# Three groups of routed pairs instead of two, tile sums on GpSimd, and a last chunk spread over all of PSUM, in a two-layer transformer kernel

## The chip, the cores and the metric

One core of a Trainium2 chip runs the whole program. The metric is the device time of one execution in microseconds; lower is better. The engines of the core are TensorE (PE in the profile, with its weight loads shown as PEld), VectorE (DVE), ScalarE (ACT), GpSimd (POOL) and SyncE (SP, which here only issues transfers). Each engine works through its own list of instructions in order.

## The reference, cut to what matters

The input x has 4 sequences of 1024 tokens with 256 values each, in float32. Two layers follow each other, each an attention-like part and a part with 8 experts, each part wrapped in a normalization with a scale and a shift, and added back through a gate. The change lies in layer 1:

```python
h = layernorm(x) * (1 + ca) + sa
x = x + ga * fast_weight(h)                 # chunks of 128 tokens, one after the other: the weights of
                                            # a chunk are those of the chunk before times a decay
h = layernorm(x) * (1 + cb) + sb
logits = h @ router_w.T                     # 8 experts
probs = softmax(logits); topk_vals, topk_idx = top_k(probs, 2)
topk_w = topk_vals / (topk_vals.sum(-1) + 1e-6)
expert_out = einsum('nh,eho->eno', h, expert_weights)           # 256 x 256 for each expert
x = x + gb * sum over the two chosen (expert_out[chosen] + probs[chosen]) * topk_w
```

The decay of a chunk needs the mean squared error of the chunk before, so the chunks of the fast-weight part are a chain. Only two of eight experts count for a token, so the kernel computes, for most tokens, only those two.

## The kernel before, in words

A sequence of 1024 tokens is 8 chunks of 128; a chunk has one tile of 128 tokens by 256 values for each of the 4 sequences, so layer 1 has 8 chunks of 4 tiles. For each chunk c the function `fast` computes the fast-weight part: 32 matmuls of 512 columns (`p_u`, line 2007), a SiLU on ScalarE (line 2019) and a product on VectorE (line 2023), 32 matmuls of 256 columns (`p_f`, line 2055), and per tile a step that GpSimd adds to x (line 2103). `normal` then normalizes the chunk (statistics and the modulation of line 1618 on VectorE, scaling on ScalarE at line 1608) and transposes it on TensorE (`pm_t`, line 1660). `routed` computes the 8 logits (`pm_e`, line 188; `pm_l`, line 2150) and, on VectorE, the two best experts.

Pairs of a token and a chosen expert are then sorted by expert in **groups**. Group `ga` takes chunks 0 to 3 (16 tiles), group `gb` chunks 4 to 6 (12 tiles); the last chunk, 7, is not sorted. When the last chunk of a group is routed, `closed` counts the pairs of each expert (`pm_turn`, `pm_total`, `pm_bases`, `pm_rank`, `pm_blocks` on TensorE, small operations on VectorE and ScalarE). Each expert's pairs are cut into blocks of 128 rows, with a fixed number of blocks for a group of n tiles:

```python
def blocks_of(n):
    return 2 * n + E - 1
```

That is 39 blocks for `ga` and 31 for `gb`. A block (function `block`) finds its rows (`reach`, `look` and `find`: lines 752, 765 and 778 to 787), gathers them from DRAM through an indirect transfer that GpSimd issues (`xg`, line 347), transposes them (`pm_x`, line 2298), copies them out (line 2304), multiplies them with one expert's weights (`p_e`, line 2315), copies the product out (`y`, line 2325) and stores it to DRAM on SP's queue (line 2328). When all blocks of a group are stored, `combine` gathers for each tile of the group the two products of each token (`yg`, line 347, two indirect transfers for one tile), scales the first on ScalarE (line 1544), adds the second, multiplies by the gate and adds the result to x, all three on VectorE (lines 1550, 1553 and 1555). When the four tiles of a chunk are done, SP stores the chunk (line 2503, 512 KB).

The last chunk goes through `dense`: all 8 experts for all its tokens, as 16 slots of two matmuls of 512 columns (line 2363), each slot consumed by two VectorE operations with the routing weights (lines 2379 and 2388), a gate and a sum on VectorE for each tile (lines 2408 and 2409), and a store of 128 KB for each tile (line 2412).

The PSUM memory has 8 banks, divided in three pools: `p1` of 3 banks, `p2` of 2, `pm` of 3. `dense` uses `p1` alone. Five buffers hold gathered tiles (`yg2`), four hold gathered rows (`xg`), three hold products (`y`).

The order of the instructions on each engine is written by a **planner**, the class `Plan`. Every piece of work is given an engine, an estimated cost, the pieces it comes after, the buffers it holds and a rank; `run` plays this through with the estimates, always starting the ready piece of the lowest rank, and emits the pieces in the order in which they began. A rank such as `c + 0.92` is a place in units of a chunk. On the chip each engine then follows its list in order and waits on semaphores where a piece is not ready. The ranks of the groups are written out by hand: `base, span` for the blocks of a group, a pair of numbers for the sums and the stores.

Of the kernel before, what the change touches and what calls it, by code (L numbers as in the profile page):

```python
# [12 lines left out]
ALU = mybir.AluOpType  # L13
# [20 lines left out]
STRIP = 32  # L34
AHEAD = 3
DX = D + 2
W1ROW = KD * H + KH
# [3 lines left out]
class Plan:  # L41
# [6 lines left out]

    LATENCY, PATIENCE, GRACE = 0.12, 0.4, 0.3

    def __init__(self, rings=(), **room):
# [11 lines left out]
    def run(self):  # L63
        room = dict(self.room)
        ring = {kind: [] for kind in self.rings}
        begun, ended, free, held = {}, {}, {}, []
        left = sorted(range(len(self.pieces)), key=lambda i: (self.pieces[i][5], i))
        t = 0.0
        while left:
# [13 lines left out]
            for i in list(left):  # L83
                engine, us, _, after, holds, rank, at, lag = self.pieces[i]
                if any(a not in ended for a in after):
# [3 lines left out]
                    + [  # L89
                        ended[a] + (self.LATENCY if self.pieces[a][0] != engine else 0.0)  # L90
                        for a in after
# [16 lines left out]
                for h in need:  # L108
                    h[2] = True
                    room[h[0]] -= 1  # L110
                    if h[0] in ring:
                        ring[h[0]].append(h)
                begun[i], ended[i] = t, t + us + lag
                free[engine] = t + us
                held += [(t + us + lag + self.LATENCY, i, q) for q in range(len(holds))]
                left.remove(i)
            if left:
                later += [e[0] for e in held if e[0] > t]
                later += [
                    ended[a] + self.LATENCY  # L120
                    for i in left
                    for a in self.pieces[i][3]
                    if a in ended and ended[a] + self.LATENCY > t
                ]
# [15 lines left out]
def adaln_d2_kernel(  # L140
# [1308 lines left out]
    mods1 = [l1.tile([P, B, D], F32, name=f"mod{i}") for i in range(6)]  # L1449
    groups = [Pairs(l1, l1, "ga", 4 * B), Pairs(l1, l1, "gb", 3 * B)]  # L1450
    mod_rows1 = dram.tile([B, 6, D], F32, name="mod_rows1")
# [41 lines left out]

    def combine(key, c, kind, y, g, tile_of, bias, gate, after, rank, at=0.0, stage=None):

        done = []
        for b in range(B):
# [50 lines left out]
            def second(b=b, s=s):  # L1548
                t = made[key, c, b]
                nc.vector.scalar_tensor_tensor(  # L1550
                    t[:, 0, :], t[:, 1, :], g.w[:, 1, s : s + 1], t[:, 0, :], ALU.mult, ALU.add
                )
                nc.vector.tensor_tensor(t[:, 0, :], t[:, 0, :], gate[:, b, :], ALU.mult)  # L1553
                xs = x_sb[:, c, b, :]
                nc.vector.tensor_tensor(xs, xs, t[:, 0, :], ALU.add)  # L1555

            a = plan(ACT, 0.45, first, after=[got[0]], holds=[slot], rank=rank)
            done.append(
                plan(DVE, 1.35, second, after=[got[1], a], holds=[slot], rank=rank + 0.01 * b)
            )  # L1560
        return done

# [772 lines left out]
    def dense(c, slotT, ts, d, x, rank):  # L2335
# [19 lines left out]
        for b in range(B):  # L2355
            last, st = [], plan.slot("step")
            for j in range(E // 2):
                ps = plan.slot("p1")

                def mm(b=b, j=j):  # L2360
                    p1 = made[key, b, j] = psum(ps_1, [P, 2, D], "p1_e")
                    for k in range(KD):
                        nc.tensor.matmul(  # L2363
                            p1,
                            lhsT=made["n2", c, "hT"][:, k, b, :],
                            rhs=ew[:, 2 * j : 2 * j + 2, k, :],
                            start=(k == 0),
                            stop=(k == KD - 1),
                        )
# [47 lines left out]
    last_pairs = Pairs(l1, l1, "gc", B)  # L2417
    lasts = {"decay": [], 0: [], 1: []}
# [3 lines left out]
    stored = {0: [], 1: []}  # L2422
    for g, rows in zip(groups, rows_of):
        for k in range(KD):
            nc.sync.dma_start(rows[g.n * P :, k * P : (k + 1) * P], ones[:1, :])
    for c in range(NC):
# [3 lines left out]
        else:  # L2430
# [18 lines left out]
        slot, slotT, hs, ts = normal(  # L2449
            ("n2", c), c, "2", [[d] for d in sums], (SHB, SCB), 7.65 if c == NC - 1 else c + 0.92, [range(B)]  # L2450
        )
        which = 0 if c < 4 else 1
        if c == NC - 1:
            d, x = routed(last_pairs, c, 0, slotT, ts, 7.46)
            dense(c, slotT, ts, d, x, 8.23)
            continue
        g, first = groups[which], 4 * which
        at = (c - first) * B
# [12 lines left out]
        )  # L2471
        if c in (3, 6):
            lists, experts, slots = closed(g, lasts[which], c + 0.97)
            base, span = ([4.57, 1.5], [7.35, 0.66])[which]
            ys = [
# [12 lines left out]
            for q in range(first, c + 1):  # L2488
# [9 lines left out]
                    [*ys, slots],  # L2498
                    (6.49, 7.89)[which] + 0.2 * (q - first),
                )  # L2500
# [67 lines left out]
```

## Time and profile before

| what | value |
|---|---|
| runs shown | 1120.11 us median of 3 (1119.87 to 1120.88) |
| profiled execution | 1141.97 us, of which the span from first to last instruction is 1140.2 us |
| mean granted TensorE clock in it | 0.986 |
| PE busy | 1086.3 us, 95% of the span |
| DVE busy | 592.0 us, 52% |
| ACT busy | 428.6 us, 38% |
| POOL busy | 422.5 us, 37% |
| last matmul ends | 1126.4 us after the span's start |

The profiled execution is 21.9 us (2.0%) longer than the median of the runs without a profile. Durations below come from that one execution, so sums are made against its span of 1140.2 us.

In the profile a line such as "L347 POOL DMA_INDIRECT" is a group of instructions of one source line on one engine; "[4.21 <-remote]" behind an instruction is the time that its engine sat idle ahead of it, and what ended the wait. "remote" and "another core or an unknown queue" mean that the recorded events name no releaser. For an indirect transfer the duration is the time in which GpSimd issues it, not the time until the data has landed.

### The profile page before, as it was taken

The numbers are of one execution on the slowest core, as the hardware profiler recorded it, in microseconds if no ns is written. First come the engines' busy times: TensorE is split into PE (matmuls) and PEld (weight loads), VectorE is DVE, ScalarE is ACT, GpSimd is POOL, SyncE is SP. The second block draws the span as 40 slices with busy tenths as digits, with TensorE's granted clock in tenths as the row PEclk, the third lists the DMA queues.
The fourth block names the chain that finished last, engine by engine and source line by source line (L and its number), as shares of the span: only waits on it lengthen the run. The fifth ranks groups of instructions, "written<-read, shape, count | busy, mean of one in ns | idle before, by whom it ended". The sixth has DMA issues, their size and how long they took to land. (4 is left out here: it accounts for less than half of the span.)

```text
span 1140.2 us, 18501 instructions
## 1 busy us (share of the span) xinstructions
PE 1086.3 (95%) x6238; PEld 847.0 (74%) x6238; DVE 592.0 (52%) x2308; ACT 428.6 (38%) x1164; POOL 422.5 (37%) x483
## 2 busy tenths in 40 slices
PE   8998999999999999999999999999999999899883
PEld 5894999999999999999988466566576575547641
DVE  7787232222222222222274788975776445888456
ACT  5976333322333323233343343432434235333421
POOL 1000455555555555555543011010044233616452
PEclk8999999999999999999999999999999999999996
DMA  9414549242422415151260312100024223323532
GB/s 321 174 31 103 191 156 302 100 153 75 154 78 75 150 39 192 33 193 40 70 223 27 96 34 83 39 10 19 19 62 129 75 82 103 102 88 107 155 118 93
DMA packets 77693, 122.38 MB, mean 107 GB/s; under 512 B 27340, under 2 KB 57301, under 8 KB 72990
## 3 DMA queue, kind: packets, MB, share of 16 engines
q0 software_dynamic: 31872, 69.68, 19.5%
q1 hardware_dynamic: 44622, 49.92, 13.3%
q10 hardware_dynamic: 1104, 1.58, 0.4%
q8 instruction: 52, 0.85, 0.3%
q14 instruction: 43, 0.35, 0.1%
HBM read 205.25 MB, written 30.22 MB: 207 GB/s over the span
## 5 line engine op out<-in xcount | busy, mean ns | idle before, releaser
L1710 ACT ACTIVATE hid<-p_h,w 128x128 f32<-128x128 f32 x544 | 154.8, 368 | 323.5 <-issue 251.9
L1698 PEld LDWEIGHTS p_h<-xT,w 128*128 128x128 f32 x2176 | 253.2, 192 | 7.2 <-DVE xT L1683 1.9
L1698 PE MATMUL p_h<-xT,w 128*128 128x128 f32 x2176 | 254.7, 275 | 3.1 <-DVE xT L1683 2.7
L1721 PE MATMUL p_y<-w,hid 128*128 128x256 f32 x1088 | 249.0, 382 | 0.2 <-issue 0.2
L2007 PE MATMUL p_u<-hT,a 128*128 128x512 f32 x512 | 232.0, 596 | 2.9 <-ACT hf L2019 1.4
L1721 PEld LDWEIGHTS p_y<-w,hid 128*128 128x128 f32 x1088 | 201.6, 190 | 25.1 <-DMA w<-in_W,g_wrow 0.4
L2007 PEld LDWEIGHTS p_u<-hT,a 128*128 128x128 f32 x512 | 93.5, 190 | 100.5 <-issue 89.7
L347 POOL DMA_INDIRECT w<-in_W,g_wrow x134 | 135.1, 1008 | 77.4 <-ACT hid L1710 46.7
L1683 DVE COPY xT<-pm_x 128x256 f32<-128x256 f32 x68 | 28.8, 424 | 187.0 <-PE pm_x L1678 134.4
L812 POOL DMA_INDIRECT y<-y,g_dest x68 | 69.5, 1022 | 143.5 <-DVE g_reached L752 108.4
L2055 PE MATMUL p_f<-a,hf 128*128 128x256 f32 x512 | 116.7, 380 | 2.0 <-DVE step L2096 1.0
L1732 DVE TENSOR_TENSOR y<-p_y,w 128x256 f32<-128x256 f32 x68 | 28.9, 425 | 166.9 <-PE p_y L1721 160.7
L2055 PEld LDWEIGHTS p_f<-a,hf 128*128 128x128 f32 x512 | 95.9, 190 | 20.8 <-issue 5.9
L347 POOL DMA_INDIRECT xg<-h_rows,g_row x68 | 66.7, 980 | 120.4 <-DVE g_row L787 98.9
L2103 POOL TENSOR_TENSOR x_sb<-x_sb,step 128x256 f32<-128x256 f32 x32 | 24.9, 778 | 205.8 <-DVE step L2096 153.6
L2315 PE MATMUL p_e<-ew,xT 128*128 x280 | 71.5, 386 | 0.8 <-ACT y L2325 0.8
L2019 ACT ACTIVATE hf<-p_u,decay 128x512 f32<-128x512 f32 x56 | 38.2, 685 | 74.9 <-PE p_u L2007 63.5
L347 POOL DMA_INDIRECT xg<-ga_rows,ga_row x39 | 37.3, 956 | 54.1 <-DVE g_hits L778 19.3
L2315 PEld LDWEIGHTS p_e<-ew,xT 128*128 128x128 f32 x280 | 49.0, 190 | 11.0 <-issue 3.8
L2023 DVE SCALAR_TENSOR_TENSOR hf<-p_u,decay,hf 128x512 f32<-128x512 f32 x56 | 41.9, 748 | 25.7 <-PE p_u L2007 14.3
L1618 DVE TENSOR_TENSOR h<-h,mod 128x256 f32<-128x256 f32 x128 | 51.6, 425 | 6.8 <-ACT h L1608 4.1
L2325 ACT COPY y<-p_e 128x256 f32<-128x256 f32 x70 | 26.1, 373 | 51.4 <-PE p_e L2315 19.2
(371 smaller groups left out, 1259.1 us busy)
## 6 DMA issues: line engine op xcount, KB each, us to landing
yg<-y SPq DMA_DIRECT2D x32, 256.0 KB
ga_y<-y SPq DMA_DIRECT2D x39, 128.0 KB
x_sb<-in_x SPq DMA_DIRECT2D x8, 512.0 KB
h_rows<-xn SPq DMA_DIRECT2D x8, 512.0 KB
gb_y<-y SPq DMA_DIRECT2D x31, 128.0 KB
out_x<-x_sb SPq DMA_DIRECT2D x7, 512.0 KB
a<-in_fw SPq DMA_DIRECT2D x6, 512.0 KB
mod<-mod_rows SPq DMA_DIRECT2D x6, 512.0 KB
```

The lines of the kernel that those rows point to most:

```text
L347: return nc.gpsimd.indirect_dma_start(out=dst, out_offset=None, in_=table, in_offset=bass.IndirectOffsetOnAxis(ap=index, axis=0), bounds_c ...
L812: nc.gpsimd.indirect_dma_start(out=table, out_offset=bass.IndirectOffsetOnAxis(ap=dest, axis=0), in_=y, in_offset=None, bounds_check=2 * s ...
L1618: nc.vector.tensor_tensor(h, h, mods1[(sc, sh)[i]][:, b, :], (ALU.mult, ALU.add)[i])
L1698: nc.tensor.matmul(p1[:, i, :], lhsT=w1[:, k * H + m * P : k * H + (m + 1) * P], rhs=xT[:, k, :], start=(k == 0), stop=(k == KD - 1),)
L1710: nc.scalar.activation(hid[:, m, :], p1[:, i, :], AF.Relu, bias=w1buf[j % 2][:, KD * H + m : KD * H + m + 1],)
L1721: nc.tensor.matmul(p2, lhsT=hid[:, m, :], rhs=w2[:, m * D : (m + 1) * D], start=(m == 0), stop=(m == KH - 1),)
L1732: nc.vector.tensor_tensor(y, p2, w2buf[j % 2][:, KH * D :], ALU.add)
L2007: nc.tensor.matmul(pu, lhsT=a[:, k, m * P : (m + 1) * P], rhs=made["n1", c, "hT"][:, k, :, :], start=(k == 0), stop=(k == KD - 1),)
L2019: nc.scalar.activation(made[key, m], made[key, m, 0], AF.Silu, scale=decays[c])
L2023: nc.vector.scalar_tensor_tensor(h, made[key, m, 1], decays[c], h, ALU.mult, ALU.mult)
L2055: nc.tensor.matmul(made[key, "p2", b], lhsT=made[key, m][:, b * P : (b + 1) * P], rhs=a1[:, m, :], start=(m == 0), stop=(m == KH - 1),)
L2315: nc.tensor.matmul(made[key, "p2"], lhsT=made[key, "xT"][:, k, :], rhs=ew_flat[:, bass.ds(made[key, "at"] + k * D, D)], start=(k == 0), st ...
```

## The change

Five things change, all in layer 1 or in the planner:

1. **Groups.** Chunks 4 to 6 become two groups: `gb` with chunks 4 and 5 (8 tiles, 23 blocks) and `gd` with chunk 6 alone (4 tiles, 15 blocks). There are 77 blocks in place of 70, and a third call of `closed`.
2. **Sums on GpSimd.** In `combine` for layer 1's groups the last addition to x (line 1555) moves from VectorE to GpSimd, as a planned piece of its own; the tile's `yg` buffer is held until it is done.
3. **Last chunk.** The 16 slots of `dense` take their banks in turn from `p1`, `p2` and `pm`.
4. **Ranks.** The ranks of blocks, sums, stores and of the last chunk are replaced by new numbers.
5. **Late messages.** The planner keeps for each piece a time at which the other engines see its end (`seen`). After three or more gathers in a row on GpSimd, a piece of TensorE that ends while they run is taken to be seen later, by 0.5 us for each gather of the row. This alters the planned order only; it adds no instruction.

The diff, cut to its core:

```diff
+N2_LAST, ROUTE_LAST, DENSE = 7.373, 6.892, 8.748
+BLOCKS = ((4.449, 1.589), (6.583, 0.614), (7.627, 0.308))
+SUMS = (6.672, 7.642, 8.45)
+STORES = (5.708, 7.465, 8.095)
+GROUPS = ((0, 1, 2, 3), (4, 5), (6,))
...
+    GATHER, APART, MANY = 1.28, 0.5, 3
...
-                        ended[a] + (self.LATENCY if self.pieces[a][0] != engine else 0.0)
+                        seen[a] + self.LATENCY if self.pieces[a][0] != engine else ended[a]
...
+                seen[i] = ended[i]
+                if engine == "POOL" and us == self.GATHER:
+                    row = row + 1 if t < fetched + self.APART else 1
+                    fetched = t + us
+                elif engine == "PE" and row >= self.MANY and t + us < fetched + self.GATHER:
+                    seen[i] += 0.5 * row
...
-    groups = [Pairs(l1, l1, "ga", 4 * B), Pairs(l1, l1, "gb", 3 * B)]
+    groups = [Pairs(l1, l1, name, len(of) * B) for name, of in zip(("ga", "gb", "gd"), GROUPS)]
...
+        def add(engine, b):
+            xs = x_sb[:, c, b, :]
+            engine.tensor_tensor(xs, xs, made[key, c, b][:, 0, :], ALU.add)
...
                 nc.vector.tensor_tensor(t[:, 0, :], t[:, 0, :], gate[:, b, :], ALU.mult)
-                xs = x_sb[:, c, b, :]
-                nc.vector.tensor_tensor(xs, xs, t[:, 0, :], ALU.add)
+                if y is None:
+                    add(nc.vector, b)
...
-            done.append(
-                plan(DVE, 1.35, second, after=[got[1], a], holds=[slot], rank=rank + 0.01 * b)
-            )
+            d = plan(
+                DVE,
+                1.35 if y is None else 0.93,
+                second,
+                after=[got[1], a],
+                holds=[slot],
+                rank=rank + 0.01 * b,
+            )
+            if y is not None:
+                d = plan(
+                    POOL,
+                    0.76,
+                    lambda b=b: add(nc.gpsimd, b),
+                    after=[d],
+                    holds=[slot],
+                    rank=rank - 0.5,
+                )
+            done.append(d)
...
-                ps = plan.slot("p1")
+                kind = ("p1", "p2", "pm")[(b * E // 2 + j) % 3]
+                ps = plan.slot(kind)
 
-                def mm(b=b, j=j):
-                    p1 = made[key, b, j] = psum(ps_1, [P, 2, D], "p1_e")
+                def mm(b=b, j=j, kind=kind):
+                    bank = {"p1": ps_1, "p2": ps_2, "pm": ps_m}[kind]
+                    p1 = made[key, b, j] = psum(bank, [P, 2, D], f"{kind}_d")
...
-        which = 0 if c < 4 else 1
         if c == NC - 1:
-            d, x = routed(last_pairs, c, 0, slotT, ts, 7.46)
-            dense(c, slotT, ts, d, x, 8.23)
+            d, x = routed(last_pairs, c, 0, slotT, ts, ROUTE_LAST)
+            dense(c, slotT, ts, d, x, DENSE)
             continue
-        g, first = groups[which], 4 * which
+        which = [c in of for of in GROUPS].index(True)
+        g, first = groups[which], GROUPS[which][0]
...
-        if c in (3, 6):
+        if c == GROUPS[which][-1]:
             lists, experts, slots = closed(g, lasts[which], c + 0.97)
-            base, span = ([4.57, 1.5], [7.35, 0.66])[which]
+            base, span = BLOCKS[which]
...
-                    (6.49, 7.89)[which] + 0.2 * (q - first),
+                    SUMS[which] + 0.2 * (q - first),
...
-                plan(SP, 0.1, store, after=done, rank=(6.4, 8.2)[which] + 0.2 * (q - first))
+                plan(SP, 0.1, store, after=done, rank=STORES[which] + 0.2 * (q - first))
```

In the program that the planner writes, TensorE's list is the same up to chunk 4's second half of `p_f`. From there on the blocks of `ga` lie a little differently; the 23 blocks of `gb` lie among the matmuls of chunks 6 and 7 in place of 31 blocks among and behind those of chunk 7; the 15 blocks of `gd` lie among and behind the last `p_f` of chunk 7; and 15 of the 16 dense slots stand at the very end in one row. On GpSimd the 32 gathers of `ga`'s tiles, which stood in one stretch between the row gathers of `ga` and of `gb`, are mixed with the row gathers of `gb`'s blocks and with the new additions; 16 gathers for `gb`'s tiles lie ahead of, among and behind the gathers of `gd`'s rows, and 8 for `gd`'s tiles come last. On SP's queue the stores of finished chunks stand between the stores of block products.

More of the change, by code (lines that the diff above doesn't have):

```diff
@@ L65, in run @@
         ring = {kind: [] for kind in self.rings}
-        begun, ended, free, held = {}, {}, {}, []
+        begun, ended, seen, free, held = {}, {}, {}, {}, []
+        fetched, row = 0.0, 0
         left = sorted(range(len(self.pieces)), key=lambda i: (self.pieces[i][5], i))
@@ L113, in run @@
                 begun[i], ended[i] = t, t + us + lag
+                seen[i] = ended[i]
[4 more added lines that the diff above has]
+                    seen[i] += 0.5 * row
                 free[engine] = t + us
-                held += [(t + us + lag + self.LATENCY, i, q) for q in range(len(holds))]
+                held += [(seen[i] + self.LATENCY, i, q) for q in range(len(holds))]
                 left.remove(i)
@@ L119, in run @@
                 later += [
-                    ended[a] + self.LATENCY
+                    seen[a] + self.LATENCY
                     for i in left
                     for a in self.pieces[i][3]
-                    if a in ended and ended[a] + self.LATENCY > t
+                    if a in seen and seen[a] + self.LATENCY > t
                 ]
@@ L2417, in adaln_d2_kernel @@
     last_pairs = Pairs(l1, l1, "gc", B)
-    lasts = {"decay": [], 0: [], 1: []}
+    lasts = {"decay": [], **{i: [] for i in range(len(GROUPS))}}
     y_of = [dram.tile([g.J * P, D], F32, name=f"{g.name}_y") for g in groups]
@@ L2421, in adaln_d2_kernel @@
     vbs = [l1.tile([P, g.n], F32, name=f"{g.name}_vb") for g in groups]
-    stored = {0: [], 1: []}
+    stored = {i: [] for i in range(len(GROUPS))}
     for g, rows in zip(groups, rows_of):
@@ L2449, in adaln_d2_kernel @@
         slot, slotT, hs, ts = normal(
-            ("n2", c), c, "2", [[d] for d in sums], (SHB, SCB), 7.65 if c == NC - 1 else c + 0.92, [range(B)]
+            ("n2", c), c, "2", [[d] for d in sums], (SHB, SCB), N2_LAST if c == NC - 1 else c + 0.92, [range(B)]
         )
-        which = 0 if c < 4 else 1
         if c == NC - 1:
-            d, x = routed(last_pairs, c, 0, slotT, ts, 7.46)
-            dense(c, slotT, ts, d, x, 8.23)
+            d, x = routed(last_pairs, c, 0, slotT, ts, ROUTE_LAST)
+            dense(c, slotT, ts, d, x, DENSE)
             continue
-        g, first = groups[which], 4 * which
+        which = [c in of for of in GROUPS].index(True)
+        g, first = groups[which], GROUPS[which][0]
         at = (c - first) * B
```

## The prediction

> **What bounds the kernel now.** I read the busy line of the page first, then busy time by stage, then the instructions of the last stages in order of time. I cut stages where TensorE transposes the logits of chunks 5, 6 and 7 (`pm_l`: 959.6, 1012.6 and 1075.7 us), because both programs have these marks. Columns: stretch, its length, then busy us and instructions of PE, PEld, DVE, ACT, POOL, then PE clock, DMA share, GB/s.
>
> ```profile
> PE 1086.3 (95%) x6238; PEld 847.0 (74%) x6238; DVE 592.0 (52%) x2308; ACT 428.6 (38%) x1164; POOL 422.5 (37%) x483
> ```
>
> ```profile
> 848.50:939.90 91.40, 88.31 (x398) 59.63 (x396) 49.01 (x215) 34.99 (x95) 34.19 (x37) 1.00 0.34 98
> 939.90:959.60 19.70, 19.21 (x89) 11.77 (x88) 11.84 (x38) 11.97 (x27) 3.97 (x5) 1.00 0.33 106
> ...
> 1012.60:1075.70 63.10, 56.17 (x288) 39.64 (x286) 42.91 (x215) 23.07 (x68) 30.52 (x33) 1.00 0.38 112
> 1075.70:1126.40 50.70, 42.60 (x113) 21.14 (x113) 29.40 (x83) 12.46 (x29) 25.00 (x26) 0.87 0.38 107
> 1126.40:1140.20 13.80, 0.00 (x0) 0.00 (x0) 8.73 (x22) 0.60 (x1) 0.23 (x1) 0.63 0.33 110
> ```
>
> TensorE bounds all but the end: it is busy 97% of both stretches to 959.6. In the last 64.5 us it has only 42.6 us of work and stops 13.8 us early. The engines in order of time (start, length, engine, line, operation, count, idle before) show why:
>
> ```profile
> 1088.01 19.05 PE L2363 MATMUL p_e<-ew,hT 128*128 128x512 f32 x44
> 1110.78 3.75 PE L2363 MATMUL p_e<-ew,hT 128*128 128x512 f32 x4 [3.72 <-issue]
> 1117.80 6.28 PE L2363 MATMUL p_e<-ew,hT 128*128 128x512 f32 x8 [3.27 <-DVE step L2388]
> ```
>
> ```profile
> 1091.07 0.94 POOL L347 DMA_INDIRECT yg<-gb_y,gb_slot  x1 [10.57 <-DMA gb_y<-y]
> ...
> 1112.79 0.95 POOL L347 DMA_INDIRECT yg<-gb_y,gb_slot  x1 [0.30 <-issue]
> 1119.24 0.94 POOL L347 DMA_INDIRECT yg<-gb_y,gb_slot  x1 [5.51 <-DVE x_sb L1555]
> ```
>
> ```profile
> 1109.63 1.00 DVE L2388 SCALAR_TENSOR_TENSOR step<-p_e,d_w,step 128x256 f32<-128x256 f32 x2 [4.21 <-remote]
> 1116.65 1.00 DVE L2388 SCALAR_TENSOR_TENSOR step<-p_e,d_w,step 128x256 f32<-128x256 f32 x2 [6.02 <-remote]
> ```
>
> ```profile
> 1135.60 0.38 SPq L2503 DMA_DIRECT2D out_x<-x_sb  x1
> ```
>
> The 24 gathers of `gb`'s tiles can start only at 1091.07, when the last of 31 blocks is stored; at 1.25 us each (0.95 and 0.30 of issue) they need 30 us, and each tile then takes VectorE 1.35 us between dense slots. VectorE waits 4.21 and 6.02 us for dense slots whose matmuls lie inside the row that ends at 1107.06: TensorE's messages come late while GpSimd issues 18 gathers in a row. TensorE, three banks ahead at most, idles 3.72 and 3.27 us and then runs at about half clock (3.75 us for a slot that takes 1.72).
>
> **What the Trainium skill says.** "TensorE: Matmul & The Clock Gate", What's actually happening: after an idle window of about 3.4 us the clock falls to half; the trace agrees (gap of 3.72 us, 0.63 granted). "Perfetto Trace Analysis", Tensor Engine Instruction: a matmul's end is a model, and its message to other engines lies outside the window; that fits waits that name no releaser, but says nothing of gathers as their cause. "SBUF — State Buffer", Who interferes with whom: a VectorE operation with two SBUF inputs and a GpSimd operation that reads SBUF exclude each other; line 2103's additions, the same shape as the new ones, take 721 to 977 ns (median 732), which agrees.
>
> **The change, part by part.** Unit prices of TensorE from its rows and the chain of waits: a 512-column matmul 0.87 us (1.74 for two), a 256-column one 0.435, a transpose 0.11, a `look` 0.06.
>
> *Seven more blocks* cost on TensorE 7 x (0.87 + 0.22 + 0.06) = 8.1 us, the third `closed` about 0.4: **+8.5 us, on the path** where TensorE bounds. On GpSimd 7 x 1.25 = 8.8; ScalarE 7 x 0.6 = 4.2; VectorE 7 x 0.8 = 5.6 and some 4 for `closed`; SP seven stores at 0.32. These four lie beside TensorE, which has 111 us in chunks 5 to 7 against some 96 of VectorE and 54 of ScalarE, counted in the same way. If that cover went, VectorE would be next.
>
> *Sums on GpSimd*: 28 times 0.42 leaves VectorE (-11.8 us) and 28 times 0.78 comes to GpSimd (+21.8). In the end stage the four for `gd` leave VectorE's path; elsewhere it gains nothing. Each is a new wait in GpSimd's list, on VectorE's line 1553; row gathers (`xg`) and further `yg` gathers queue behind it, and TensorE's `pm_x` waits for these. Bounds: nothing if VectorE is prompt; 28 waits of about 1.5 us (what a VectorE stretch such as a normalization's root lasts) on the other side. I take nothing while GpSimd has slack, computed next.
>
> *GpSimd's list* from the first `ga` tile (954.4, unchanged, since all of `ga` must be stored) to the last `gd` row gather: 32 of `ga`, 23 rows of `gb`, 10 of `gb`'s tiles, 15 rows of `gd`, 80 gathers by 1.25, and 8 steps and 20 sums by 0.78: 122 us, to 1076, plus some 4 us until `gb`'s lists are known: 1080. TensorE will want that last row at about 1095 (worked out below: the mark at 1091 and a few blocks): 15 us of slack.
>
> *SP's queue*: stores of chunks (0.38) now stand between product stores; a chunk store late for a sum holds products behind it, and three `y` buffers then stop ScalarE's copies. Taken at nothing, since `ga`'s sums come many blocks ahead; 0 to 3 us. The two one-row stores for `gd` at the start lie beside layer 0's work: nothing.
>
> *TensorE by stage*, counting the order: before, 46.9 us of work from chunk 5's `pm_l` to chunk 6's (took 53.0), 51.3 to chunk 7's (63.1), 37.0 after it. After: 63.9, 47.4 and 32.4, 143.7 against 135.2, which is the 8.5 again. Up to chunk 5's mark the sums are equal (123.4 against 123.4), so 959.6 stays. Time over work was 116.1 / 98.2 = 1.18 between the marks of chunks 5 and 7. With **the same 1.18**, 111.3 us of work take 131.4: chunk 7's mark moves from 1075.7 to **1091.0**. Not knowing how the new interleaving packs, I bound the ratio by 1.10 (more matmuls to fill in) and 1.28.
>
> *The end stage*: after that mark 6.3 us of blocks and the first dense slot, then 15 slots by 1.74 = 26.1, and 1.5 for waits: matmuls end at 1124.9. Every slot's bank now has six or more slots before it is needed again, about 10 us, which covers one late message of the size seen. VectorE needs 1.0 for a slot and 0.9 for a tile's end, less than TensorE's 1.74 a slot. The last slot's two operations (1.0), gate and sum (0.86), then a 128 KB store (2.4, as the last `gb_y` store at 1088.7 to the gather it released at 1091.07, and 0.3 of issue): **1129.5**. Beside it the last `gd` product has landed about 1102 (1091.0 + 6.3 + 1.5, copy 0.4, store 2.4); 8 gathers (10.0), 4 sums (3.1), the last pair's landing, scaling and product (3.2) and some 4 us of waits take it to 1122.3, a 512 KB store of 4.6 (1135.60 to the end) to 1126.9, under 3 us short of the path. Were the dense slots quicker, that chain would be next.
>
> Sum: 1129.5 - 1140.2 = -10.7 us of the profiled span (the execution has 1.8 us around it). The runs' median is 21.9 us under the profiled time, and some of the late messages may be smaller there; I take -10: **1110 us**.
>
> **Rivals.**
> - *GpSimd becomes the bound (slower).* Place: the stretch of `gb` and `gd` blocks. If each of 20 sums ahead of the last `gd` row stops its queue by w, the last row comes at 1080 + 20 w. It decides from w = 0.75 us (1095) and has eaten the gain at w = 1.3. At 1.6 us: 1112, 17 late, end 1146.5, +6.3: 1126.4 in the runs. For it: 122 us of work in 141, and GpSimd already waited 5.51 us for line 1555. Against: ready gathers and few waits above 2 us in `ga`'s stretch.
> - *Eaten.* The ratio between the marks rises to 1.28, as late messages still strike mid-chunk (before, ScalarE and VectorE waited up to 6.5 us in `ga`'s row of gathers). 142.5 us, mark 1102.1, end 1140.6: 1120, no change.
> - *Better packing.* Ratio 1.10: mark 1082.0, end 1120.5, -19.7: 1100. For it: `gb`'s blocks get chunk 6's matmuls as filling, where 27 of its 31 blocks before had none, from 1046 on.
> - *The change not as said*: dense slots held by busy `p2` and `pm` banks. The last three blocks hold two or three banks for at most 2 us at the start: no more than 2 us.
>
> **How the numbers follow.** The forecast (1104 to 1116 by itself) has 0.55, better packing 0.14, eaten 0.11, GpSimd bound 0.20. A measurement of this kernel tells about 0.2%, 2.2 us, from no change. Faster: 0.55 + 0.14 + 0.03 of the eaten case = 0.72; same 0.05; slower 0.20 + 0.03 = 0.23. The range 1099 to 1127 takes in the ratio of 1.10 below and the slow rival's 1126.4 above; about 0.05 lies under it and 0.13 over.
>
> **What would show it.** Right: chunk 7's `pm_l` near 1091, dense slots in one row of about 26 us at full clock, the last matmul under 4 us ahead of the last VectorE sum, the last issue a 128 KB store. Wrong: GpSimd idle ahead of `xg` gathers behind line 1511's sums for over 13 us in all, chunk 7's mark past 1101, or VectorE waiting over 10 us for dense slots. A mark before chunk 5's transposition that moved would break the equal start.

## Result: 0.7% slower where the kernel before takes 1120 us, 1.0% faster where it takes 1142 us

Beside the kernel before, in the same batch of runs, the changed kernel takes 1127.88 us (median of 4, 1127.04 to 1129.91) against 1119.99 (4 runs, 1118.66 to 1120.88): **ratio 1.0071, interval 1.0055 to 1.0088**. The forecast of 1110 us, faster, was wrong; the range ended at 1127.

The unaltered kernel before takes about 1121 us in some batches and about 1142 us in others (a batch is one set of runs on one chip, one after the other). It is no matter of the chip: chip 7 gave 1141.15 in one batch and 1121.03 in another. I call the batches **quick** and **late**, and compare only within one. The profile shown ahead of the prediction is of the late kind, the runs beside it of the quick kind.

| kernel | quick batch | late batch |
|---|---|---|
| before, median of the batch | 1119.99, 1120.78, 1121.03 | 1141.15, 1142.29, 1142.64 |
| changed kernel | 1127.88 (ratio 1.0071), 1128.26 (1.0069) | 1130.21 (0.9899) |

### The profile after

The page's busy line of the changed kernel; the profiled execution took 1127.04 us, its span 1125.2:

```profile
PE 1093.8 (97%) x6296; PEld 856.7 (76%) x6296; DVE 592.9 (53%) x2335; ACT 431.4 (38%) x1181; POOL 450.4 (40%) x518
```

Busy time by stage of the changed kernel, cut at the same marks (`pm_l` of chunks 5, 6, 7 at 956.84, 1027.75 and 1084.66, then the last matmul's end at 1118.20; the second cut lies 1.65 us behind its mark); columns as before:

```profile
956.90:1029.40 72.50, 71.40 (x307) 45.38 (x306) 53.46 (x209) 27.94 (x74) 52.06 (x57) 1.00 0.45 131
1029.40:1084.70 55.30, 51.30 (x231) 33.63 (x230) 41.78 (x168) 23.09 (x63) 42.99 (x49) 0.99 0.51 139
1084.70:1118.00 33.30, 33.24 (x88) 16.71 (x86) 26.94 (x77) 7.28 (x17) 19.36 (x22) 0.97 0.38 114
1118.00:1125.20 7.20, 0.20 (x1) 0.00 (x0) 3.73 (x9) 0.00 (x0) 0.00 (x0) 0.70 0.33 109
```

The kernel before once more, unaltered, in a quick batch (run e1_before_again, span 1120.5; marks 959.61, 1006.47, 1065.42):

```profile
959.70:1006.50 46.80, 46.80 (x165) 27.16 (x164) 40.98 (x119) 19.67 (x40) 29.91 (x32) 1.00 0.41 127
1006.50:1065.40 58.90, 54.76 (x288) 40.13 (x287) 42.85 (x214) 23.11 (x67) 31.18 (x33) 1.00 0.39 116
1065.40:1107.90 42.50, 39.39 (x114) 20.14 (x112) 30.64 (x86) 11.86 (x28) 22.45 (x24) 0.96 0.46 125
1107.90:1120.50 12.60, 0.01 (x1) 0.00 (x0) 7.49 (x19) 1.30 (x3) 3.12 (x4) 0.64 0.47 149
```

This is the base that the prediction lacked. Against it, counted from mark to mark, the changed kernel reaches chunk 5's mark 2.8 us earlier, takes 24.0 more to chunk 6's, 2.0 less to chunk 7's, 8.9 less from there to the last matmul and 5.6 less for the tail: -2.8 + 24.0 - 2.0 - 8.9 - 5.6 = +4.7, the difference of the spans. The runs differ by some 7 to 8, since e1's profiled execution lies 1.3 above its median and the other 0.8 under its own.

The end stage is as it was drawn. TensorE in order of time (start, length, engine, line, operation, count, idle before), the dense slots in one row:

```profile
1092.29 1.88 PE L2397 MATMUL p_d<-ew,hT 128*128 128x512 f32 x4
...
1116.32 1.88 PE L2397 MATMUL p_d<-ew,hT 128*128 128x512 f32 x4
```

VectorE's last sum, and SP's last two issues, a 128 KB store each:

```profile
1121.69 0.42 DVE L2443 TENSOR_TENSOR x_sb<-x_sb,step 128x256 f32<-128x256 f32 x1
```

```profile
1118.10 4.38 SPq L2446 DMA_DIRECT2D out_x<-x_sb  x2
```

The row of slots takes 25.9 us without a gap, and no wait in the trace is put down to "remote".

### Where 20 us of the kernel before come and go

The same program, two executions. VectorE in the late profile shown before, then in e1's:

```profile
971.52 0.75 DVE L2023 SCALAR_TENSOR_TENSOR hf<-p_u,decay,hf 128x512 f32<-128x512 f32 x1 [6.54 <-remote]
```

```profile
965.15 0.75 DVE L2023 SCALAR_TENSOR_TENSOR hf<-p_u,decay,hf 128x512 f32<-128x512 f32 x1 [1.76 <-PE p_u L2007]
```

And GpSimd in the same two, late first:

```profile
954.41 0.96 POOL L347 DMA_INDIRECT yg<-ga_y,ga_slot  x1 [15.77 <-DMA ga_y<-y]
...
968.17 0.94 POOL L347 DMA_INDIRECT yg<-ga_y,ga_slot  x1 [0.30 <-issue]
973.85 0.94 POOL L347 DMA_INDIRECT yg<-ga_y,ga_slot  x1 [4.74 <-DVE x_sb L1555]
```

```profile
954.42 0.96 POOL L347 DMA_INDIRECT yg<-ga_y,ga_slot  x1 [15.78 <-issue]
...
968.33 1.01 POOL L347 DMA_INDIRECT yg<-ga_y,ga_slot  x1 [0.31 <-issue]
969.64 0.95 POOL L347 DMA_INDIRECT yg<-ga_y,ga_slot  x1 [0.30 <-DVE rdown L2194]
```

At 954.4 the two still agree to 0.01 us. Then GpSimd issues a row of gathers. In the quick execution VectorE waits 1.8 us for `p_u` and the row runs through 19 gathers. In the late one the message, TensorE's signal that `p_u` is done, comes at 971.5, 2.4 us after the row has ended at 969.1 for want of free buffers: VectorE, which had to free them, was itself waiting. ScalarE, too, waits until 971.51, for 3.01 us. In e1 no wait is put down to "remote" at all; a row of 24 gathers from 1081.4 to 1111.9 passes with the dense slots beside it. The late stages are longer by 6.1 (53.0 against 46.9), 4.2 (63.1, 58.9) and 9.4 us (64.5, 55.1), 19.7 in all: the whole difference of the spans.

The updates of TensorE's semaphore, which the trace records with their times, show that the messages themselves are late, and not only what waits for them. In e1 each comes about 0.02 us after the end of its matmul, in rows of gathers too. In the late execution the matmuls that end at 963.31, 965.03, 966.85 and 969.93 have none until 971.43, 971.49 and 971.55. Over this whole trace 272 of the 621 messages whose matmul ends during a gather, or within 0.35 us of one, come over 0.1 us late, and 21 of the 630 others; in e1 it is 1 of 626 and none of 625. The message need not wait for the row's end: one of the dense slots comes at 1109.60, inside the row of 18 that ends at 1113.7. Every trace of a late batch has such messages from layer 0 on, and no trace of a quick batch has them there, so the kind is no matter of layer 1's order.

### The profile page after: what moved, and what is told of

The parts are those of the page before. It is cut to its first block, busy times and chain, and to the rows that moved or that the text cites. A ratio compares the mean times of both kernels' runs of the same rounds, so it can differ in the third digit from the quotient of the medians.

```text
span 1125.2 us, 18769 instructions
## 1 busy us (share of the span) xinstructions
PE 1093.8 (97%) x6296; PEld 856.7 (76%) x6296; DVE 592.9 (53%) x2335; ACT 431.4 (38%) x1181; POOL 450.4 (40%) x518
## 4 chain that ended last, share of the span: by engine, by line
PE 76%; DVE 10%; DMA 5%; POOL 3%; issue 3%; ACT 3%; DVEq 0%; SPq 0%; ACTq 0%; POOLq 0%
PE p_h L1730 21%; PE p_y L1753 20%; PE p_u L2039 17%; PE p_f L2087 9%; PE p_e L2347 2%; DMA w<-in_W,g_wrow 1%; PE pm_x L1710 1%; POOL yg L360 1%; POOL xg L360 1%; PE pm_counts L778 1%; PE pm_x L2330 1%; PE pm_t L1692 1%; DMA yg<-y 1%; ACT xn L1015 1%; ACT h2T L1060 1%
## 5 line engine op out<-in xcount | busy, mean ns | idle before, releaser
L2347 PE MATMUL p_e<-ew,xT 128*128 x308 | 77.9, 388 | 0.8 <-ACT y L2357 0.8
L2347 PEld LDWEIGHTS p_e<-ew,xT 128*128 128x128 f32 x308 | 55.5, 193 | 12.7 <-issue 3.6
L2055 DVE SCALAR_TENSOR_TENSOR hf<-p_u,decay,hf 128x512 f32<-128x512 f32 x56 | 41.9, 748 | 18.1 <-PE p_u L2039 13.1
```

The costliest lines, as they stand in the source:

```text
L2055: nc.vector.scalar_tensor_tensor(h, made[key, m, 1], decays[c], h, ALU.mult, ALU.mult)
L2347: nc.tensor.matmul(made[key, "p2"], lhsT=made[key, "xT"][:, k, :], rhs=ew_flat[:, bass.ds(made[key, "at"] + k * D, D)], start=(k == 0), st ...
```

## Experiments

### Quick batch (before 1120.78, 31 runs)

**e1_before_again**: no edit. 1120.87 us (20 runs), ratio 1.0001 (0.9993 to 1.0009).

> The kernel before, unchanged, to get a second profile of it. Theory A (the profiled execution of 1141.97 us was unlike the runs: late messages of TensorE during the row of 18 gathers, then the clock drop, cost about 20 us that most executions do not pay): the new profile spans 1117 to 1120 us, chunk 7's pm_l comes before 1072, the waits of 4 and 6 us of VectorE for dense slots are absent or under 2 us, and the dense slots run at full clock. Theory B (any profile of this kernel is some 20 us longer than its runs, because recording slows it): the span is 1138 to 1142 again with the same waits, while the times stay at 1120.

It settles that the kernel before can run without late messages; its trace is used above.

**e2_two_groups**: the changed kernel with the groups and ranks of before.

```diff
-BLOCKS = ((4.449, 1.589), (6.583, 0.614), (7.627, 0.308))
-GROUPS = ((0, 1, 2, 3), (4, 5), (6,))
+BLOCKS = ((4.57, 1.5), (7.35, 0.66))
+GROUPS = ((0, 1, 2, 3), (4, 5, 6))
...
```

> The changed kernel with two groups and the old ranks: sums on GpSimd, all banks for the last chunk and the late messages in the planner stay; 70 blocks. Theory A1 (what costs time in the runs is the work of 7 more blocks and a third closing, 8.5 us on a TensorE that is busy all the time): 1112 to 1121 us, that is at or under the kernel before, 7 to 15 us under the changed one. Theory A2 (the waits of the sums in GpSimd's queue cost it): 1125 us or more.

1144.35, ratio 1.0211 (1.0184 to 1.0238). TensorE ends at 1106.8, but the span is 1142.8. The waits of the trace from 950 us on (engine, tile, line, releaser: total, times, longest) and GpSimd's first and last instruction of the end:

```profile
POOL x_sb L1511 <- DVE yg L1570: 22.0, 20, 5.0
DVE yg L1567 <- DMA yg<-gb_y,gb_slot: 19.4, 10, 5.1
```

```profile
1087.45 1.06 POOL L360 DMA_INDIRECT yg<-gb_y,gb_slot  x1 [13.58 <-DMA gb_y<-y]
...
1134.79 0.72 POOL L1511 TENSOR_TENSOR x_sb<-x_sb,yg 128x256 f32<-128x256 f32 x1 [1.76 <-DVE yg L1570]
```

From its first gather to the last sum e2 needs 48.1 us, with 12 sums on GpSimd among the 24 gathers; in e1, with the sums on VectorE, the same stretch takes 34.4 (1081.38 to 1115.79). A sum on GpSimd is dear where GpSimd's list sets the end; the third group leaves only `gd`'s 4 for the very end. The 23.6 us of the whole run are not the price of the sums: the stretch also starts 6.1 us later than in e1, and e2 has the planner's edit with the old ranks, which without any sum on GpSimd costs 21.7 us (g1 below).

**e3_groups_only**: the three groups and the new ranks, without sums on GpSimd, without the other banks, and no message planned late.

```diff
-                    seen[i] += 0.5 * row
+                    seen[i] += 0.0 * row
...
-                    POOL,
-                    0.76,
-                    lambda b=b: add(nc.gpsimd, b),
+                    DVE,
+                    0.42,
+                    lambda b=b: add(nc.vector, b),
...
-                kind = ("p1", "p2", "pm")[(b * E // 2 + j) % 3]
-                ps = plan.slot(kind)
+                ps = plan.slot("p1")
```

> Three groups with their ranks alone: sums on VectorE, the last chunk in p1 alone, no late messages in the planner. Theory A1 (blocks): 1125 to 1133 us, as the 8.5 us of work are there and nothing is gained from the banks. Theory A2 (sums on GpSimd cost): under 1122 us.

1133.36, ratio 1.0118 (1.0092 to 1.0144): the groups alone lose more than the whole change.

**e4_banks_only**: the kernel before with the 16 slots taking their banks in turn from the three pools, as in the change.

> The kernel before with only the dense slots spread over p1, p2 and pm. If the row of dense slots is what ends late in ordinary runs of the kernel before (three slots ahead at most): 1108 to 1116 us. If in those runs the 24 gathers of gb's tiles and VectorE's sums behind them set the end, the banks bring under 2 us: 1118 to 1120.

1121.18, ratio 1.0000 (0.9988 to 1.0012). The slots end 3.3 us earlier than in e1 and the end stays: it is set by the row of 24 gathers and the sums behind it.

### Late batch (before 1141.15, 17 runs)

**e5_sums_on_vector**, **e6_one_pool**, **e7_no_late_messages**: the changed kernel with the sums planned on VectorE; with the dense slots in `p1` alone; with no message planned late (the three hunks shown under e3, one at a time).

> The changed kernel with one part undone: the 28 sums of combined tiles are planned on VectorE (0.42 us each) instead of GpSimd; three groups, all banks and late messages in the planner stay. Theory A1 (the 8.5 us of added TensorE work are the loss; in the changed kernel only four sums stand in the end stage, so the sums matter little): 1124 to 1131 us. Theory A2 (the sums that stop GpSimd's queue, 16 us of waits in all, are the loss): 1119 us or less.

> The changed kernel with one part undone: the last chunk's slots use the three p1 banks alone. Theory A1: the dense slots run at VectorE's pace with its waits for gathers in between, so TensorE ends later: 1129 to 1135 us. If the banks bring nothing here either (as they brought nothing to the kernel before): 1127 to 1129.

> The changed kernel with one part undone: the planner takes no message as late (0.0 us for each gather of a row in place of 0.5). Theory A1: the order changes in details only, 1124 to 1132 us. If planning for late messages that mostly do not come is what makes the order loose (the slack of 1.20 in chunk 7's stretch): 1122 us or less.

1156.76 (ratio 1.0136, 1.0102 to 1.0171), 1132.36 (0.9920, 0.9890 to 0.9949) and 1139.78 (0.9988, 0.9975 to 1.0001). The first two read together: without sums on GpSimd "remote" waits of 9.5, 6.2 and 5.9 us appear, with them none above 1.5. The longest unbroken row of gathers is 16 in e5, 6 in e6 and 7 in e7. The planner's edit is worth about 0.9%, read across two late batches (e7's 0.9988 against 0.9899 for the changed kernel, f1 below), through the order alone; e7 shows no "remote" wait either.

**e8_seventy_blocks**: the changed kernel with 3 blocks of `gb` and 4 of `gd` left out; rows routed there come out as fillings.

> The changed kernel with the last 3 blocks of gb and the last 4 of gd left out (their products in DRAM are filled with a row of another table, so pairs in them get wrong values): 70 blocks in place of 77, everything else kept. Theory A1 (the added blocks' TensorE work is the loss, 7 x 1.15 = 8 us): 1118 to 1121 us, that is the time of the kernel before. Theory A2 (waits in GpSimd's queue, not TensorE's work): 1124 us or more, since the 28 sums and their waits stay.

1133.60, ratio 0.9927 (0.9906 to 0.9949). Run again beside the changed kernel below.

### Second late batch (before 1142.29, 17 runs)

**f1_after_again** (no edit) and **f2_seventy_blocks_again** (as e8):

> The changed kernel, nothing altered, to learn its time where the kernel before takes about 1120.8 us and where it takes about 1141.2 us (two chips so far, the same program). Theory (the change trades late messages of TensorE for 8 us of further work): about 1127.5 us on either chip, so a ratio of about 1.007 where before takes 1120.8 and about 0.99 (0.985 to 0.994) where it takes 1141. Rival (the second chip is slower by 1.8% for any program): 1127.5 on the first and about 1148 on the second, a ratio of 1.006 on both.

> The changed kernel with the last 3 blocks of gb and the last 4 of gd left out, so 70 blocks as before the change; rows of tokens routed to these blocks come out as fillings. To be read against the changed kernel in the same batch. Theory (the loss is TensorE's extra work): 7 blocks by 1.15 us on the path, so 7 to 9 us below the changed kernel, about 1119.5 where before takes 1120.8 (ratio 0.999). Rival (the loss lies in how the new order packs): 3 us or less below it, ratio 1.004 or more there. Where before takes 1141 a run of this kernel gave 1133.6; if the blocks are worth 8 us there too, the changed kernel takes about 1141 there.

1130.21, ratio 0.9899 (0.9880 to 0.9919), and 1134.31, ratio 0.9927 (0.9908 to 0.9945). The changed kernel gains 1.0% here. The expectations put the two kinds down to two chips; the next quick batch, on a chip that had given a late one, refutes that. Seven blocks less are not faster but 4.1 us slower, with a "remote" wait of 9.8 us (e8 has one of 9.9): leaving blocks out moves the plan, so this run can't price them.

**f3_straight_loads**: in the kernel before, one straight transfer in place of a tile's two gathers, for layer 1's groups; the rows that are summed are then not those of the tokens.

```diff
+            def straight(b=b, s=s):
+                t = made[key, c, b] = buf(kind, [P, 2, D])
+                rows = y[2 * s * P : 2 * (s + 1) * P, :]
+                nc.sync.dma_start(t, rows.rearrange("(p i) d -> p i d", i=2))
```

> The kernel before with the two indirect gathers of each tile of layer 1's sums replaced by one straight transfer of 256 KB on SP's queue, so the rows that are summed are not those of the tokens; GpSimd's 56 gathers of tiles are gone, all else stays. Theory (the rows of gathers make the end stage long, and on one of the chips they also make TensorE's messages late): about 1113 us on either chip, so a ratio of 0.993 where before takes 1120.8 and 0.976 where it takes 1141. Rival 1 (the end is bound by VectorE's and TensorE's own work): 1119 to 1121, ratio 0.999 on the first. Rival 2 (the second chip is slow for another reason): the ratio is the same on both chips, about 0.993, and waits that name no releaser stay.

1126.68, ratio 0.9871 (0.9850 to 0.9893), and no "remote" wait: the long waits go when the gathers of tiles go. Late messages remain around the other gathers (251 of 584), but nothing waits long for them. Of some 27 us expected 15.6 came; one loss is seen, six tile ends in a row on VectorE ahead of a dense slot, for which TensorE waits 6.67 us.

**f4_store_by_tile**: in the kernel before, chunk 6 stored by tiles.

```diff
+                if q == NC - 2:
+                    for b in range(B):
+                        plan(SP, 0.1, lambda b=b: store_tile(b), after=[done[b]], rank=8.6)
+                    continue
```

> The kernel before with chunk 6 stored tile by tile (four stores of 128 KB, each after its tile's sum) in place of one store of 512 KB at the very end. Theory: the last issue is then a 128 KB store, 2.4 us to land against 4.6, so about 2 us less, 1118.6 where before takes 1120.8, ratio 0.998 (0.9965 to 0.9995). Rival (the last store's cost is fixed and not its size): no difference.

1140.75, ratio 0.9982 (0.9968 to 0.9996), as expected. It is the one edit of the kernel before that gained and kept the result, and the gain is small.

### Quick batch again (before 1121.03, 9 runs)

**g1_planner_only** (the kernel before with the `seen` lines of the diff) and **g2_planner_banks_tiles** (with e4's and f4's edits besides):

> The kernel before with the planner's late messages alone: two groups, sums on VectorE, dense slots in p1, old ranks; no instruction is added, only the order differs. Theory A (that edit is what makes the changed kernel steady): where before takes 1141 to 1142, some 10 us less, ratio 0.991, and no waits over 4 us that name no releaser; where before takes 1120.8, 0 to 3 us more. Theory B (the new split into groups does it, with its blocks among matmuls that need no row of gathers): ratio 0.997 to 1.003 on either chip, and such waits stay.

> The kernel before with the late messages in the planner, the dense slots over all PSUM banks and chunk 6 stored tile by tile; two groups, sums on VectorE. Theory A (late messages of dense slots cost the kernel before its last 20 us, and more banks let TensorE run on through them): where before takes 1141 to 1142, about 1123, ratio 0.984, below the changed kernel's 1130; where before takes 1120.8, about 1118, ratio 0.9975. Theory B (the banks and the planner do nothing without the new groups): the tile stores' 2 us alone, ratio 0.998.

1142.70, ratio 1.0187 (1.0172 to 1.0203), and 1139.41, ratio 1.0166 (1.0150 to 1.0182): both theories missed. The first gather of `gb`'s tiles comes at 1100.85 in g1 where e1 has it at 1081.38, and the same row of 24 gathers ends the kernel. No "remote" wait stands in either trace. The hand-written ranks belong to one planner; its edit with the old ranks puts the last blocks, and so the gathers behind them, late.

**g3_half_products**, with **g4_after_again** as its base:

```diff
-            for k in range(KD):
+            halves = 1 if g.name in ("gb", "gd") and j % 2 == 0 else KD
+            for k in range(halves):
```

> The changed kernel with the second of the two matmuls left out in every second block of gb and gd (12 and 8 blocks), so those products are of half the sum; the order is the same and nothing else is left out. It takes 20 by 0.435 = 8.7 us of work from TensorE, as much as the seven extra blocks and the third closing added. To be read against the changed kernel in the same batch. Theory (TensorE bounds those stages, one to one): 7 to 9 us below it. Rival (GpSimd's list of gathers and sums sets when blocks can be multiplied): under 3 us below it.

> The changed kernel unaltered, as the base for the run with half products, and to see once more how its time stands where before takes 1120.8 (theory: ratio 1.006 to 1.008) or 1141 to 1142 (0.988 to 0.992).

1128.87 (ratio 1.0081, 1.0065 to 1.0097) against 1128.26 (1.0069, 1.0056 to 1.0083). **Taking 8.7 us of work from TensorE gives nothing.** Stage by stage, half products first:

```profile
956.30:1027.30 71.00, 66.96 (x281) 40.20 (x279) 50.12 (x206) 27.80 (x74) 52.46 (x56) 1.00 0.46 131
1027.30:1085.10 57.80, 49.09 (x220) 31.16 (x219) 42.89 (x170) 23.07 (x63) 43.27 (x48) 1.00 0.49 133
```

```profile
955.50:1026.50 71.00, 69.95 (x299) 44.00 (x297) 50.26 (x206) 28.07 (x74) 52.41 (x56) 1.00 0.45 131
1026.50:1083.90 57.40, 52.41 (x239) 34.61 (x238) 43.08 (x170) 23.04 (x63) 43.23 (x49) 1.00 0.50 137
```

TensorE's busy time falls and no stage gets shorter. GpSimd is a candidate: in the second of g4's stages it is busy 43.23 of 57.4 us, and the gaps of issue ahead of its gathers, none over 0.31 us, add 9.1 that the busy figure leaves out: 52.4, or 91%. In the first it is 63.4 of 71.0, or 89%. In e1 the same second stage has 31.2 + 8.3 = 39.5 of 58.9. The rest are waits, 6.0 us of them (both stages) for VectorE ahead of the sums of line 1511, so VectorE, and the landing of gathers, are rivals that g3 does not rule out. TensorE waits for gathered rows around the end of the second stage, from 1026 to 1090 2.2 us in g4 and 4.1 us in g3; one of g4's waits:

```profile
1087.14 0.41 PE L2330 MATMUL pm_x<-ident,xg 128*128 128x128 f32 x2 [1.30 <-DMA xg<-gd_rows,gd_row]
```

### Third late batch (before 1142.64, 32 runs)

**h1_sums_in_place**, and **h2_in_place_half** with g3's edit on top:

```diff
-                    lambda b=b: add(nc.gpsimd, b),
+                    lambda b=b: add(nc.gpsimd if g.name == "gd" else nc.vector, b),
```

> The changed kernel, planned as it is, but the 24 sums of the tiles of ga and gb are issued on VectorE at the place where the plan begins them on GpSimd (gd's 4 stay); the lists of TensorE and ScalarE are the same, GpSimd's list loses 24 additions. Theory (GpSimd's list of gathers and sums paces the changed kernel up to the last row gather of gd: taking 8.7 us from TensorE gave nothing): GpSimd loses 24 by 0.87 = 21 us and the waits of the sums for VectorE, TensorE becomes the bound after some 5 to 10 us, so 1118 to 1123 where the changed kernel takes 1128 (before 1121), ratio to before 0.997 to 1.002 there; 1121 to 1126, ratio 0.981 to 0.986, where before takes 1141 to 1142. Rival (VectorE's chain of scaling, adding and gates paces it, or the landing of gathers): no gain, or a loss of up to 5 us, since VectorE gets 10 us more.

> The run with 24 sums issued on VectorE in place, and besides the second matmul left out in every second block of gb and gd, so those products are half sums (20 by 0.435 = 8.7 us off TensorE, which gave nothing in the changed kernel itself). Theory (with GpSimd relieved TensorE is the bound): 4 to 8 us below the run with the sums in place. Rival (the bound is still elsewhere, GpSimd's gathers alone or VectorE): under 2 us below it.

1156.06 (11 runs from 1142.96 to 1160.02), ratio 1.0093 (1.0061 to 1.0125), and 1145.73, ratio 1.0024 (1.0013 to 1.0036). Both theories missed: late messages came. The lists of TensorE and ScalarE are those of the changed kernel; only 24 additions left GpSimd's, for VectorE's. GpSimd, ScalarE and TensorE of h1:

```profile
1035.04 0.94 POOL L360 DMA_INDIRECT xg<-gb_rows,gb_row  x1 [0.30 <-PE pm_e L201]
...
1046.34 0.95 POOL L360 DMA_INDIRECT yg<-ga_y,ga_slot  x1 [0.30 <-issue]
```

```profile
1048.57 0.27 ACT L2178 COPY le<-pm_e 128x128 f32<-128x128 f32 x1 [13.12 <-remote]
```

```profile
1048.89 0.48 PE L2182 MATMUL pm_l<-ident,le 128*128 128x128 f32 x1 [11.30 <-ACT le L2178]
```

`pm_e` is multiplied from 1033.94 on, in 0.64 us; its message reaches ScalarE at 1048.6, 1.3 us after a row of 14 gathers has ended at 1047.3. Around 1110 it happens again (10.80 us, a row of 11). In the changed kernel the sums cut these rows: its longest is 7, in the late f1 it is 6, and no "remote" wait there is above 1.8 us. So **in this plan the additions between the gathers, each with its wait for VectorE, keep the waits for late messages short**. The messages are late in f1 as well, 264 of the 662 in or near a gather. Additions alone are not enough: e8 and f2 keep all 28, have no row over 7, and VectorE still waits 9.9 and 9.8 us for `p_u`. In e8 rows of 7 and 5 gathers stand ahead, with one addition between them that waited for nothing:

```profile
1026.72 0.74 POOL L1511 TENSOR_TENSOR x_sb<-x_sb,yg 128x256 f32<-128x256 f32 x1
```

```profile
DVE hf L2055 <- remote: 9.9, 1, 9.9
```

As a test of GpSimd as the bound h1 failed, since its batch brought late messages; h2 against h1 (-10.3 us) moved them too and decides nothing.

## Why the prediction was wrong, point by point

1. **The step that failed is the last of the sum**: "The runs' median is 21.9 us under the profiled time, and some of the late messages may be smaller there; I take -10". The 21.9 us were the late messages themselves: the profiled execution was of the late kind, the runs of the quick kind. The gain of 10.7 us was worked out of waits that the runs shown did not have. Where they have them, the change gave 1142.29 to 1130.21, -12.1 us, close to the -10.7 of the sum, though its parts missed in opposite directions there (f1: chunk 7's mark at 1086.4 and not 1091.0, from there 40.7 us and not 38.5), so some of the closeness is luck. The text saw the 21.9 and named late messages, but took an offset for what was a second kind of execution.
2. *The changed kernel's own span*: 1129.5 predicted, 1125.2 measured, even too long. The ratio of 1.18 carried over held late messages: in e1 it is 105.8 / 98.2 = 1.08, after the change 127.8 / 111.3 = 1.15. Chunk 7's mark came at 1084.7, not 1091.0. The mark of chunk 5, taken as unmoved, came 2.8 us earlier. Even on the right base the sum would have missed: e1's own 1.08 puts chunk 7's mark at 1079.8 and the end at 1118.3, 2.2 us faster than e1, where the changed kernel is 4.7 slower. So the second step that failed is "the same 1.18", a ratio that the new order was to keep: it rose from 1.08 to 1.15, some 8 us over 111.3 us of work.
3. *+8.5 us on the path*: the term lies near the 7 to 8 us that the runs lost, but g3 shows that in the changed kernel TensorE's work is not what paces these stages, so the nearness proves nothing.
4. *GpSimd's list*: 122 us of it, to 1080, was well sized; the last row gather was issued at 1083.4. The 15 us of slack were not there, because TensorE was 6.3 us earlier than assumed and asked for that row among its next blocks. The slow rival's mechanism, a full GpSimd, fits the traces (some 90% of both stages in g4) at a smaller price than it named: the sums ahead of that row wait some 6 us in all for VectorE, far under 20 times 0.75. That GpSimd is the bound is argued from this and g3, not shown by a run that relieves it.
5. *The end stage*: right in its shape. One row of slots (26.1 predicted, 25.9), last matmul 3.5 us ahead of the last VectorE sum's start, 128 KB stores last. The cover of "six or more slots" for a late message was never needed in quick batches, and e4 shows the banks alone at nothing.
6. *Sums costed at nothing*: wrong in both directions. They fill GpSimd's list (in e2 the stretch with 12 of them is 13.7 us longer than e1's), and in this plan they break its rows, which in late batches is worth some 26 us (h1, 1156.06, against f1, 1130.21).

What the Trainium skill says: "Perfetto Trace Analysis", DMA Instruction — SWDGE (GPSIMD), has the window of such a transfer end when its descriptors are generated, not when data has moved. The traces agree: 0.95 us of window, where the first gather of `ga`'s tiles is waited for until 4.03 us after its start (chain of waits of g4). The same page, Identifying the Most-Contended Engine, takes occupancy as a fair measure for GpSimd; here the page of the profile shows 40% for an engine that in g4 is 91% taken in a stage that did not get shorter, once the stage is cut out and the gaps of issue are added. Its word in Tensor Engine Instruction (MATMUL, LD_WEIGHTS), that a matmul's message lies outside the profiled window, fits the waits without a releaser; that such messages come late around gathers no page states. The prediction's 0.63 is the clock granted behind the last matmul; the slot of 3.75 us itself was granted 0.50. In e1 a gap of 2.00 us was followed by half clock too (a slot of 3.40 us, 0.50 granted from 1106.0 to 1107.9), shorter than the window of 3.4 us that the prediction takes from the skill.

What stays open: why a batch is quick or late; what paces the changed kernel's stages, GpSimd, VectorE or the landing of gathers; whether a GpSimd list without the 24 additions would pay in a quick batch; and a version that beats both kernels in both kinds, which none of these runs is. In late batches the changed kernel had the best ratio of all complete ones, in quick batches the kernel before was not beaten.

## What to carry to other kernels

Before a gain is subtracted from the runs' median, make sure that the profiled execution belongs to the same kind of run: a profile 2% over the runs with waits that name no releaser is another case, not the same case with an offset, and the waits that it shows may not be there to be won. Judge an engine that issues transfers by its stage, with the issue time added, and not by its share of the span. Ranks written by hand belong to one planner and one set of pieces; parts of such a change can't be priced one at a time (e2, e3, g1: 1.0211, 1.0118, 1.0187 for parts of a change of 1.0071).

## What the hardware showed that was not expected

In late batches completion messages of TensorE came late around GpSimd's indirect gathers, some inside a row and some 1.3 to 2.4 us after its end (rows of 14 and 12), with up to 13.1 us of wait. In quick batches rows of 19 and 24 delayed nothing, with the same program. In the changed kernel's late run, with rows of up to 6 cut by additions of 0.73 us and their waits, no wait for such a message was over 1.8 us; rows of 7 and 5 with one addition between them did cost 9.9 us (e8). In e2 the last 24 gathers with 12 additions of 128 x 256 on GpSimd took, from the first gather to the last sum, 13.7 us more than in e1 with the additions on VectorE; the additions themselves are 8.6 us of that.
